# The last two token groups of a feed-forward kernel: their statistics, the flag's test and the last stores put in another order on the vector engine

## The chip, the cores and the metric

The kernel runs on one core of one Trainium2 chip. The metric is the device time of one execution in microseconds (us); less is better. The core has a matrix engine (PE), a vector engine (DVE), an activation engine (ACT), a general engine (POOL) and a synchronisation engine (SP), which here only issues transfers. Each takes its own instructions in order; they wait for one another through semaphores.

## The reference

The input is 4096 tokens of 256 numbers. Cut to what matters:

```python
x = layernorm(x + attn(x))        # linear attention, D = 64
h = silu(x @ w1.T * s1) * (x @ w2.T * s2)     # 256 -> 1024
h = gelu(h @ h1.T * hs1)                      # 1024 -> 1024, exact gelu
h = gelu(h @ h2.T * hs2)
x = layernorm(x + (h @ w3.T) * s3)            # 1024 -> 256; this is the output
```

A layernorm here subtracts the mean of a token's 256 numbers and divides by the root of their variance plus 1e-5. There is no learned scale or shift.

## The kernel before, in words

The tokens are cut into eight tiles of 512, and these are worked on in four pairs. A tile has four groups of 128 tokens (`NS` = 4); within a group a token lies on a partition and its 256 features along the row. Products are made in two parts, of a rounded matrix `hi` and the remainder `lo`, and the square layers use a seven-product scheme. The matrix engine is kept busy with these products from the start to within some 8 us of the end. The program is written out by hand in order: there is no scheduler that moves instructions, so the order of calls in the source is each engine's order.

The change lies in the last stretch, after the last pair's products (`ta` and `tb` are its two tiles). For each group `s` of a tile the work is:

- `last_products` (line 900) makes the group's 128x256 product with `w3` in a PSUM bank;
- `scaled` (line 909) multiplies the bank with `s3` into a tile `d` on the vector engine;
- an addition puts `d` on the residual row `x2[t][:, s, :]`;
- `statistics` (lines 150 and 152) takes mean and variance into `mvo`;
- a reciprocal root of the variance is made. For most groups it is `rstd_of` (lines 87 and 88, with a power on POOL). For the last two groups it is `root_on_act` (lines 1152 and 1153): a square root on ACT, then four small vector steps (reciprocal, and one Newton step of three instructions), which the caller places one by one;
- the row is normalised, either by two ACT instructions (minus the mean, times the root) or by one vector instruction, and stored by `store` (line 1164), a transfer on SP's queue.

The last two groups are `y` (tile `tb`, group 2) and `u` (tile `tb`, group 3). `y` is normalised on ACT (lines 1210 and 1220), `u` on the vector engine (line 1232). Each has a store of its own of 128 KB.

Among these steps stands the end of a test. `within` (lines 1020 and 1021) sets `ok` for the last eight groups' variances, a reduction (line 1225) takes the least of all `ok`, a matrix product with ones (line 1228) adds this over the partitions, and line 1231 turns the sum into `flag`. Four engines load `flag` (line 1234) and branch (line 1240): if it were set, a general program would run again from the start. In the runs here it isn't set.

Of the kernel before, what the change touches and what calls it, by code (L numbers as in the profile page):

```python
# [11 lines left out]
F32 = mybir.dt.float32  # L12
# [4 lines left out]
ALU = mybir.AluOpType  # L17
AX = mybir.AxisListType
# [3 lines left out]
P = 128  # L22
# [8 lines left out]
NS = T // P  # L31
# [13 lines left out]
def block_kernel(ctx: ExitStack, tc: tile.TileContext, a: dict, out: bass.AP):  # L45
# [15 lines left out]
    nc = tc.nc  # L61
# [3 lines left out]
    def const(name, shape, dt=F32):  # L65
        return cp.tile(shape, dt, tag=name, name=name)

    s1 = const("s1", [P, KH])
# [7 lines left out]
    ones = const("ones", [P, 1])  # L76
# [5 lines left out]
    flag = const("flag", [1, 1], I32)  # L82
# [14 lines left out]
    p2 = fast.enter_context(tc.tile_pool(name="two", bufs=2))  # L97
    p3 = fast.enter_context(tc.tile_pool(name="three", bufs=3))

    bank = [bp.tile([P, T], F32, tag=f"bank{i}", name=f"bank{i}") for i in range(8)]  # L100
# [21 lines left out]
    x2 = {}  # L122
# [24 lines left out]
    def norm_stats(us, mv, s0):  # L147
        st = p2.tile([P, 2, 6], F32, tag="bn", name="bn")
        for j, u in enumerate(us):
            nc.vector.bn_stats(st[:, j, :], u)  # L150
        for j in range(len(us)):
            nc.vector.bn_aggr(mv[:, s0 + j, :], st[:, j, :])
# [331 lines left out]
    def sums(layer, k, raw):  # L484
# [20 lines left out]
        def first():  # L505
            plus(v[0], a21, a22)
            plus(v[1], v[0].bitcast(F32), a11, ALU.subtract)
            store(0)

        def second():  # L510
            plus(v[2], a11, a21, ALU.subtract)
            plus(v[3], a12, v[1].bitcast(F32), ALU.subtract)
            store(1)
# [23 lines left out]
    for c in (slice(0, H // 2), slice(H // 2, H)):  # L537
        d = nc.gpsimd.dma_start(out=w1[:, :, c], in_=a["w1"][:, :, c])
# [16 lines left out]
    for _ in range(WARM):  # L555
        nc.tensor.matmul(
            pw, nc.const_aps.tensor(1.0, [P, P], BF), nc.const_aps.tensor(1.0, [P, T], BF),
            start=True, stop=True,
# [232 lines left out]
    for i in range(2, 2 * KH):  # L791
# [13 lines left out]
        if i in (11, 14):  # L805
            t = 2 + i // 14
# [86 lines left out]
    mvo = p1.tile([P, NT * NS, 2], F32, tag="mvo", name="mvo")  # L893
# [12 lines left out]
    def scaled(t, s):  # L906
        ps = (al, be)[t % 2][s]
        d = p2.tile([P, E], F32, tag="d", name=f"d{t}", bufs=4)
        nc.vector.tensor_tensor(d, ps[:, :E], s3, ALU.mult)  # L909
        return d  # L910
# [28 lines left out]
    def end_jobs(t, engine=nc.gpsimd, queue=nc.gpsimd):  # L939
        root, norm, store = out_norm(t)  # L940

        def half(s):
            root([s, s + 1])
            for i in (s, s + 1):
                norm(i, engine)
            if s:
                store(0, NS, queue)

        return [(1.3, functools.partial(half, s)) for s in (0, 2)]
# [45 lines left out]
    low, high, fine, some = (most[:, i : i + 1] for i in range(4))  # L995
    ok = p1.tile([P, NT * NS], F32, tag="ok", name="ok")
# [21 lines left out]
    def within(dst, var, so_far):  # L1018

        nc.vector.tensor_scalar(dst, var, low, so_far, ALU.is_ge, ALU.mult)  # L1020
        nc.vector.scalar_tensor_tensor(dst, var, high, dst, ALU.is_le, ALU.mult)
# [20 lines left out]
    for p in range(NP):  # L1042
        ta, tb = 2 * p, 2 * p + 1
        if p > 0:
            first = []
            ask(1)
            for i in range(2 * KH):
# [13 lines left out]
                if p + 1 < NP and i in (6, 11):  # L1061
                    t = ta + 2 + int(i == 11)
# [77 lines left out]
    def statistics(t, ss):  # L1140
        norm_stats([x2[t][:, s, :] for s in ss], mvo[:, t * NS : (t + 1) * NS, :], ss[0])
# [6 lines left out]
    def root_on_act(t, s):  # L1148

        var, r, e = (p3.tile([P, 1], F32, tag=n, name=n) for n in ("var", "rr", "re"))  # L1150
        mv = mvo[:, t * NS + s, 1:2]
        nc.scalar.activation(r, mv, AF.Sqrt, bias=eps)
        nc.vector.tensor_scalar(var, mv, EPS, None, ALU.add)


        return r, [
            functools.partial(nc.vector.reciprocal, r, r),
            functools.partial(nc.vector.scalar_tensor_tensor, e, r, var, r, ALU.mult, ALU.mult),
            functools.partial(nc.vector.tensor_scalar, e, e, -0.5, 1.5, ALU.mult, ALU.add),
            functools.partial(nc.vector.tensor_tensor, r, r, e, ALU.mult),  # L1160
        ]

    def store(t, s0, s1):
        nc.sync.dma_start(out=out[t][:, s0:s1, :], in_=x2[t][:, s0:s1, :])

    g, v = nc.gpsimd, nc.vector
    for s in range(NS):
# [23 lines left out]
    for s in range(2):  # L1191
        norm_on_act(ta, 2 + s, *ra[s])
    store(ta, 2, 4)
    d = scaled(tb, 1)
    statistics(tb, [0])
    (r0,) = roots(tb, [0])
    y = x2[tb][:, 1, :]
# [6 lines left out]
    store(tb, 0, 2)  # L1204
    n = (NT - 1) * NS
    y, u = x2[tb][:, 2, :], x2[tb][:, 3, :]
    statistics(tb, [2])
    r, steps2 = root_on_act(tb, 2)
    (m,) = minus_mean(tb, [2])
    nc.scalar.activation(y, y, AF.Identity, bias=m, scale=1.0)  # L1210
    d = scaled(tb, 3)
    steps2[0]()
    v.tensor_tensor(u, u, d, ALU.add)
    steps2[1]()
    st = p2.tile([P, 2, 6], F32, tag="bn", name="bn")
    nc.vector.bn_stats(st[:, 0, :], u)
    steps2[2]()
    steps2[3]()
    nc.vector.bn_aggr(mvo[:, n + 3, :], st[:, 0, :])
    nc.scalar.activation(y, y, AF.Identity, scale=r)  # L1220
    store(tb, 2, 3)
    r, steps3 = root_on_act(tb, 3)
    within(ok[:, n - NS :], mvo[:, n - NS :, 1], fine)
    steps3[0]()
    nc.vector.tensor_reduce(some, ok, AX.X, ALU.min)
    steps3[1]()
    pf = bank[7][:1, :1]
    nc.tensor.matmul(pf, some, ones, start=True, stop=True)
    steps3[2]()
    steps3[3]()  # L1230
    nc.vector.tensor_scalar(flag, pf, float(P), None, ALU.is_lt)
    nc.vector.tensor_scalar(u, u, mvo[:, n + 3, 0:1], r, ALU.subtract, ALU.mult)
    store(tb, 3, 4)
    differs = nc.values_load(
        flag, engines=AGAIN, min_val=0, max_val=1,
# [178 lines left out]
```

## Time and profile before

| what | us |
|---|---|
| median of three executions | 638.31 |
| these three | 638.42, 638.31, 636.43 |
| the profiled execution, its own time | 636.66 |
| its span, first to last instruction | 634.8 |
| matrix engine busy | 623.5 |
| last large product ends, from the span's start | about 626.95 |
| last vector instruction, start and length | 630.59, 0.41 |
| last store issued by SP, start and length | 631.03, 0.33 |

The profile shows one execution. Its own time is 1.86 us above its span, which is what lies around the first and the last instruction. Engine rows give start and length, both in us from the span's start. On DVE and ACT, the next instruction can start before the one ahead of it has ended if it doesn't need its result. For SP, a row is the time in which the engine issues a transfer; the landing is told apart from it.

### The profile page before, as it was taken

How to read it: one execution, taken by the hardware profiler on the slowest of the kernel's cores; microseconds unless marked ns; L12 is line 12 of the kernel's file. 1: busy time of each engine (PE TensorE's matmuls, PEld its weight loads, DVE VectorE, ACT ScalarE, POOL GpSimd, SP SyncE). 2: the span in 40 equal slices, each digit the busy share in tenths (PEclk: the TensorE clock that was granted, in tenths of full speed). 3: DMA queues.
4: the chain of work that ended last, by engine and by line, in shares of the span. 5: the costliest groups of instructions: out<-in, count | busy, mean ns of one | idle time of the engine just before them, and what ended most of it. 6: DMA issues, size and time to landing. Idle time of an engine off the chain costs nothing.

```text
span 634.8 us, 9039 instructions
## 1 busy us (share of the span) xinstructions
PE 623.5 (98%) x3169; PEld 526.7 (83%) x3169; DVE 488.4 (77%) x767; ACT 379.2 (60%) x547; POOL 219.0 (34%) x280
## 2 busy tenths in 40 slices
PE   8999999999999999999999999999999999999995
PEld 7788888888898888888898888888898888888894
DVE  2799985889668787889668798798676796597456
ACT  5455553659845374655755457747754547765674
POOL 1343023204855409305545505603653700000043
PEclk9999999999999999999999999999999999999999
DMA  8999669978641158647741135645861035443301
GB/s 340 360 312 319 223 221 359 282 234 257 159 150 65 66 199 291 207 135 219 243 135 33 67 132 190 223 152 176 233 156 35 33 133 174 173 152 132 100 1 69
DMA packets 59409, 113.31 MB, mean 179 GB/s; under 512 B 19776, under 2 KB 34112, under 8 KB 59232
## 3 DMA queue, kind: packets, MB, share of 16 engines
q1 hardware_dynamic: 40880, 73.89, 35.1%
q0 software_dynamic: 18192, 38.41, 19.5%
q8 instruction: 26, 0.43, 0.3%
q10 hardware_dynamic: 288, 0.39, 0.2%
q14 instruction: 23, 0.19, 0.1%
HBM read 96.94 MB, written 18.87 MB: 182 GB/s over the span
## 4 chain that ended last, share of the span: by engine, by line
PE 95%; DVE 2%; DMA 1%; ACT 1%; issue 0%; POOL 0%; ACTq 0%; DVEq 0%; POOLq 0%
PE bank L305 64%; PE bank L737 18%; PE bank L900 9%; PE bank L602 1%; PE bank L140 1%; PE bank L581 1%; DMA f<-in_xt 1%; DVE so L317 0%; DVE bn L150 0%; PE bank L652 0%; PE bank L210 0%; PE bank L747 0%; ACT stk L665 0%; DVE d L909 0%; DVE stk L671 0%
## 5 line engine op out<-in xcount | busy, mean ns | idle before, releaser
L305 PE MATMUL bank<-hi,ws 128*128 128x512 f32 x896 | 348.7, 389 | 0.0
L305 PE MATMUL bank<-lo,ws 128*128 128x512 f32 x896 | 348.6, 389 | 0.0
L260 DVE TENSOR_TENSOR lo<-f,hi 128x1024 fp32r<-128x1024 f32 x142 | 168.3, 1224 | 59.6 <-ACT hi L259 59.0
L305 PEld LDWEIGHTS bank<-lo,ws 128*128 128x128 f32 x896 | 168.2, 188 | 35.0
L305 PEld LDWEIGHTS bank<-hi,ws 128*128 128x128 f32 x896 | 168.1, 188 | 34.9
L259 ACT CAST hi<-f 128x1024 fp32r<-128x1024 f32 x142 | 142.6, 1051 | 48.2 <-PE bank L305 25.1
L355 ACT ACTIVATE f<-f,hs 128x512 f32<-128x512 f32 x96 | 62.5, 715 | 68.7 <-DVE f L317 68.7
L737 PE MATMUL bank<-hi,w 128*128 128x512 f32 (+1 forms) x256 | 99.0, 388 | 0.4 <-ACT hi L218 0.4
L737 PE MATMUL bank<-lo,w 128*128 128x512 f32 (+1 forms) x256 | 98.8, 387 | 0.1
L756 ACT ACTIVATE f<-bank,s 128x512 f32<-128x512 f32 x64 | 44.1, 690 | 68.9 <-PE bank L737 66.0
L317 DVE TENSOR_TENSOR f<-f,f 128x1024 f32<-128x1024 f32 x64 | 76.5, 1221 | 4.5 <-ACT f L355 3.8
L317 DVE TENSOR_TENSOR f<-f,bank 128x512 f32<-128x512 f32 x96 | 61.4, 682 | 15.3 <-ACT f L410 11.3
L757 DVE SCALAR_TENSOR_TENSOR f<-bank,s,f 128x512 f32<-128x512 f32 x64 | 47.8, 748 | 25.2 <-PE bank L737 23.9
L900 PE MATMUL bank<-w,lo 128*128 128x256 f32 x240 | 57.9, 283 | 0.0
L900 PE MATMUL bank<-w,hi 128*128 128x256 f32 x240 | 57.9, 283 | 0.0
L737 PEld LDWEIGHTS bank<-hi,w 128*128 128x128 f32 x256 | 48.1, 188 | 10.1 <-ACT hi L218 0.6
L244 POOL DMA_DIRECT2D xT<-x x96 | 52.2, 551 | 11.7 <-DMA stage<-in_h 4.5
L737 PEld LDWEIGHTS bank<-lo,w 128*128 128x128 f32 x256 | 48.1, 188 | 9.7 <-DVE lo L219 0.3
L862 POOL DMA_DIRECT2D stage<-in_h x16 | 9.2, 575 | 127.2 <-DVE stage L888 100.4
L900 PEld LDWEIGHTS bank<-w,lo 128*128 128x128 f32 x240 | 46.1, 192 | 0.2
L900 PEld LDWEIGHTS bank<-w,hi 128*128 128x128 f32 x240 | 46.0, 192 | 0.2
L915 POOL TENSOR_TENSOR x<-x,d 128x256 f32<-128x256 f32 x29 | 25.7, 904 | 30.8 <-DVE d L909 30.7
(165 smaller groups left out, 538.4 us busy)
## 6 DMA issues: line engine op xcount, KB each, us to landing
ws<-sw SPq DMA_DIRECT2D x100, 512.0 KB, 3.4
sw<-so POOLq DMA_DIRECT2D x16, 512.0 KB, 4.9
stage<-in_h POOLq DMA_DIRECT2D x16, 512.0 KB, 5.0
ws<-in_h POOLq DMA_DIRECT2D x12, 512.0 KB, 6.6
sw<-in_h SPq DMA_DIRECT2D x12, 512.0 KB, 5.5
x<-in_x SPq DMA_DIRECT2D x16, 256.0 KB, 5.6
f<-in_xt SPq DMA_DIRECT2D x7, 512.0 KB, 7.0
f<-in_h SPq DMA_DIRECT2D x6, 512.0 KB, 7.8
```

What stands on the lines that cost most here:

```text
L244: moves.popleft()()
L259: nc.scalar.copy(hi[:, c, :], src[:, c, :])
L260: nc.vector.tensor_tensor(lo[:, c, :], src[:, c, :], hi[:, c, :].bitcast(F32), ALU.subtract)
L305: nc.tensor.matmul(ps[2 * h + o], w[:, k, o * P : (o + 1) * P], part[i][:, k, :], start=start and k == 0 and i == 0, stop=k == HK - 1 and ...
L317: engine.tensor_tensor(dst, u, v, op)
L355: nc.scalar.activation(dst, src, AF.Gelu, scale=sc[:, o : o + 1])
L737: nc.tensor.matmul(ps[:, c], w[:, k, o * P : (o + 1) * P], part[:, 2 * j + k, c], start=(k == 0 and i == 0), stop=(k == KE - 1 and i == 1),)
L756: nc.scalar.activation(g, pa, AF.Silu, scale=s1[:, o : o + 1])
L757: nc.vector.scalar_tensor_tensor(g, pb, s2[:, o : o + 1], g, ALU.mult, ALU.mult)
L862: nc.gpsimd.dma_start(out=st[:, :n], in_=src.rearrange("p k o -> p (k o)")[:, c : c + n])
L900: nc.tensor.matmul(ps[:, :E], part[q][:, k, s * P : (s + 1) * P], w3[:, k0 + k, :], start=i % 2 == 0 and k == 0 and q == 0, stop=i % 2 == ...
L915: engine.tensor_tensor(y[:, s, :], y[:, s, :], scaled(t, s), ALU.add)
```

## The change

The order of the calls for the groups `y` and `u` is rewritten. `u` is scaled and added right behind `y`'s statistics, before `y`'s root. `y`'s and `u`'s statistics get two tiles of their own, `st2` and `st3`. `u`'s square root stands ahead of `y`'s last scaling on ACT. The test (`within`, the reduction, the product) stands ahead of the small steps of the two roots, and these are interleaved. `store` gets a parameter for the queue with SP's as its default, and no call passes another one. No instruction is added or taken out on any engine; the five stores of these two tiles keep their sizes and their order.

```diff
-    def store(t, s0, s1):
-        nc.sync.dma_start(out=out[t][:, s0:s1, :], in_=x2[t][:, s0:s1, :])
+    def store(t, s0, s1, queue=nc.sync):
+        queue.dma_start(out=out[t][:, s0:s1, :], in_=x2[t][:, s0:s1, :])
...
     store(tb, 0, 2)
     n = (NT - 1) * NS
     y, u = x2[tb][:, 2, :], x2[tb][:, 3, :]
-    statistics(tb, [2])
+    st2, st3 = (p2.tile([P, 2, 6], F32, tag="bn", name="bn") for _ in range(2))
+    nc.vector.bn_stats(st2[:, 0, :], y)
+
+    d = scaled(tb, 3)
+    nc.vector.bn_aggr(mvo[:, n + 2, :], st2[:, 0, :])
+    v.tensor_tensor(u, u, d, ALU.add)
     r, steps2 = root_on_act(tb, 2)
     (m,) = minus_mean(tb, [2])
     nc.scalar.activation(y, y, AF.Identity, bias=m, scale=1.0)
-    d = scaled(tb, 3)
+    nc.vector.bn_stats(st3[:, 0, :], u)
     steps2[0]()
-    v.tensor_tensor(u, u, d, ALU.add)
+    nc.vector.bn_aggr(mvo[:, n + 3, :], st3[:, 0, :])
+    r3, steps3 = root_on_act(tb, 3)
+    within(ok[:, n - NS :], mvo[:, n - NS :, 1], fine)
+    nc.vector.tensor_reduce(some, ok, AX.X, ALU.min)
+    pf = bank[7][:1, :1]
+    nc.tensor.matmul(pf, some, ones, start=True, stop=True)
     steps2[1]()
-    st = p2.tile([P, 2, 6], F32, tag="bn", name="bn")
-    nc.vector.bn_stats(st[:, 0, :], u)
+    steps3[0]()
     steps2[2]()
+    steps3[1]()
+    nc.vector.tensor_scalar(flag, pf, float(P), None, ALU.is_lt)
     steps2[3]()
-    nc.vector.bn_aggr(mvo[:, n + 3, :], st[:, 0, :])
     nc.scalar.activation(y, y, AF.Identity, scale=r)
     store(tb, 2, 3)
-    r, steps3 = root_on_act(tb, 3)
-    within(ok[:, n - NS :], mvo[:, n - NS :, 1], fine)
-    steps3[0]()
-    nc.vector.tensor_reduce(some, ok, AX.X, ALU.min)
-    steps3[1]()
-    pf = bank[7][:1, :1]
-    nc.tensor.matmul(pf, some, ones, start=True, stop=True)
     steps3[2]()
     steps3[3]()
-    nc.vector.tensor_scalar(flag, pf, float(P), None, ALU.is_lt)
-    nc.vector.tensor_scalar(u, u, mvo[:, n + 3, 0:1], r, ALU.subtract, ALU.mult)
+    nc.vector.tensor_scalar(u, u, mvo[:, n + 3, 0:1], r3, ALU.subtract, ALU.mult)
     store(tb, 3, 4)
```

## The prediction

> **What bounds the kernel now.** I read the page first, then the chain of waits from its end backwards, then the timelines of DVE, ACT and SP after 626 us, and last the view of the store's line.
>
> ```profile
> PE 623.5 (98%) x3169; PEld 526.7 (83%) x3169; DVE 488.4 (77%) x767; ACT 379.2 (60%) x547; POOL 219.0 (34%) x280
> ...
> PE 95%; DVE 2%; DMA 1%; ACT 1%; issue 0%; POOL 0%; ACTq 0%; DVEq 0%; POOLq 0%
> ```
>
> PE is busy for 98% of the span and carries 95% of the chain. None of that moves. The change stands behind the last product, which ends near 626.95, so it works on the last 7.85 us alone. There the chain runs through DVE, with one step on ACT:
>
> ```profile
> 628.77 0.16 DVE rr L1218
> 628.93 0.10 DVE mvo L1219
> 629.04 0.50 ACT x L1220
> 629.54 0.19 ACT rr L1152
> 629.73 0.02 issue
> 629.75 0.16 DVE rr L1224
> 629.92 0.08 DVE most L1225
> 630.00 0.18 DVE re L1226
> 630.18 0.02 issue
> 630.21 0.17 DVE re L1229
> 630.37 0.02 issue
> 630.40 0.16 DVE rr L1230
> 630.56 0.06 DVE flag L1231
> 630.62 0.39 DVE x L1232
> ```
>
> The reader is to see one detour: the variance of `u` is there at 629.03, but its square root (L1152) stands on ACT behind `y`'s last scaling (L1220), so its reciprocal (L1224) starts at 629.75. The chain stops at 631.0; what follows hangs on SP. In SP's timeline and in the view of the store's line:
>
> ```profile
> 629.56 0.33 SPq L1164 DMA_DIRECT2D out<-x  x1
> ```
>
> ```profile
> 631.03 0.33 SPq L1164 DMA_DIRECT2D out<-x  x1
> DMA to landing us min/median/max: 1.8/2.0/2.0
> ```
>
> `y`'s store goes out 1.47 us ahead of `u`'s, and SP is free when `u` is ready. The lines of the load (L1234) and the branch (L1240) show SP loading the flag at 631.4, just behind this issue, and its closing semaphore waits from 632.5 to 633.1; `u`'s store lands in between, at about 632.9. Both the flag's load and the landing hang on the start of SP's last issue, 3.74 us before the span's end (634.77 less 631.03). So the time is: **start of SP's last issue plus 3.74**.
>
> **What the Trainium skill says.** "Perfetto Trace Analysis", section on the DVE and ACT instruction, says that a row ends where the write is acknowledged and the semaphore is then sent. The trace agrees: a vector instruction that needs the one ahead starts 0.03 to 0.04 after its end (626.50 to 626.53). "VectorE: DVE Perf Modes", section "The DRAIN you can't avoid", says that a next operation that isn't held starts earlier. The trace agrees: 0.33 from start to start behind a 256-wide operation (627.34 to 627.67), 0.07 to 0.08 behind a 128x1, at most 0.13 behind a three-operand one (628.14 to 628.27). "Perfetto Trace Analysis", section on HWDGE transfers, says that SP's row ends when SP is free again, without the movement; here 0.33 against 1.8 to 2.0 to landing. "DMA: Bandwidth & Descriptors", "Anatomy of one DMA", puts most of a small transfer's 2 us down to the receipt of the write; 128 KB and 256 KB landing in 1.8 and 2.0 agrees.
>
> **The change part by part.** Nothing is added: the instructions on each engine are the same in number, and so are the five stores. `queue` is SP's by default in every call, so that edit costs nothing because it changes nothing. The rest is order. I carry the rules above through the new order, with the durations of the DVE and ACT rows.
>
> 1. *`u` scaled at once.* `y`'s `bn_stats` stays at 626.53. The scaling waits for the bank, done at 626.95, so it starts at 626.97 instead of 627.34 and ends at 627.39. `y`'s aggregation goes behind it: 627.30 instead of 627.00 (+0.30). The addition to `u` needs the scaling: 627.42 to 627.85 (before, to 628.22: -0.37). Then var 627.75, minus 627.82; `u`'s `bn_stats` 627.88 to 628.31; `y`'s reciprocal 628.21; `u`'s aggregation 628.34 to 628.52 (before, to 629.03: -0.51).
> 2. *ACT.* `y`'s root at 627.52, `y` minus mean at 628.00 to 628.51, `u`'s root at 628.56 to 628.84. The detour of the chain is gone: the root no longer waits for `y`'s last scaling.
> 3. *The test goes first.* var 628.56, the two of `within` 628.63 and 628.94 to 629.17 (0.28 and 0.23, the second needs the first), reduction 629.21 to 629.37. Before they lay in DVE's wait for ACT; now they stand ahead of both roots, and this takes most of what step 2 won.
> 4. *Woven steps.* `y`'s second step 629.31; `u`'s reciprocal 629.44 to 629.60 (before 629.75: -0.31); `y`'s third 629.57 to 629.71; `u`'s second 629.64 to 629.85; flag 629.76; `y`'s root done 629.84 to 630.00 (before, to 628.93: **+1.07**); `u`'s third 629.92 to 630.07; `u`'s root 630.11 to 630.27; `u` normalised **630.30 to 630.71** (before, to 631.00: **-0.29**).
> 5. *Stores.* `y`'s scaling on ACT waits for two engines and took 0.09 to start (rr ends 628.93, ACT 629.03): 630.10 to 630.61. SP issues `y`'s store at 630.63 instead of 629.56. It is first in SP's queue, so `u`'s, ready at 630.74, waits behind it. An issue takes 0.33, and between two stores stands one semaphore check (the store's line shows two, 17 ns each), with gaps of 0.03 to 0.05: 0.43 in all. `u`'s store goes at **631.06**, against 631.03.
>
> Sum: the vector engine ends 0.29 earlier, and SP's queue gives 0.32 back: **+0.03 us**, so 636.69 for the profiled execution.
>
> Costs that the trace doesn't show. *Two stores back to back*: at least 0.38 (issue and gap alone), at most 0.65, as 0.60 issues of small blocks of xT on this queue; I take 0.43. *Landing of two close stores*: queue 1 spent 35.1% of 16 x 634.8 us on 40,880 packets, 0.087 us each at 1.8 KB; a store is 128 rows of 1 KB, 8 per DMA engine, so at most 0.70 for the first, 0.43 of it past when the second starts: 0 to 0.27 later; I take 0, since a packet here is about half the mean size. A gain I exclude: a second transfer on the same queue has no reason to land faster. *The flag's wait for PE*: behind it on DVE stand the ends of both roots, and ACT and SP behind these. Before, the flag (630.48) followed the reduction's end (630.00) with no wait visible, so PE's answer takes 0.47 at most: 629.84 against my slot of 629.76, 0 to 0.08 late; I take 0. No gain is possible there.
>
> **The rivals.** *(A) SP's queue doesn't bind.* If `y`'s root came 0.3 earlier, the store would be out of the way and the end would be DVE's: -0.29, 636.4. For it: a plain reading of the chain, which ends on DVE. Against it: step 4 puts the test and most of `u`'s steps ahead of `y`'s root. *(B) A jam on SP, slower.* Place: `u`'s store behind `y`'s. It decides once `y`'s store goes later than 630.60 (631.03 less 0.43). Price: the upper bounds, 0.08 + 0.22 + 0.27, on top of 0.03: +0.6, 637.3. If `u`'s store even had to wait for `y`'s landing: 630.63 + 1.85 + 0.03 = 632.51, +1.48, 638.1. Against that last: SP issues the small blocks of xT every 0.65 us while each lands 4.2 later, so the queue doesn't wait for landings. *(C) The change does nothing measurable and the executions' own spread decides.* The four executions shown are 636.43, 636.66, 638.31 and 638.42, 1.99 apart; every price above is smaller.
>
> **How the numbers follow.** Chances: my sum, within 0.15 of no change, 0.55; (A), 0.15; (B), 0.25 up to +0.6 and 0.05 for the landing. All but the last leave the kernel the same; (C) lies over all of them. The profiled execution is 1.65 below the median of the three. Nothing in the tail tells the two pairs apart, so I don't carry the sum to the median: I take the mean of the four executions, 637.46, plus 0.03: **637.5**. Low end 636.43 less 0.23, most of (A): 636.2. High end 638.42 plus 0.4, most of (B): 638.8. Beyond these lie at most 2 in 10. A difference of about 0.3%, 1.9 us, is what a measurement of this kernel can tell from no change. To be faster by that, the median must fall under 636.4: the lower pair with a part of (A), 0.20. To be slower it must pass 640.2: the upper pair with the landing of (B) and more, 0.08. The same: 0.72.
>
> **What would show it.** Right: the last vector row ends near 630.7; `u`'s root on ACT stands ahead of `y`'s scaling; `y`'s store starts near 630.6 and `u`'s 0.4 behind it, near 631.05; the span stays at 634.8 within 0.2. Wrong: `u`'s store with a gap ahead of it on SP (A); an issue gap over 0.65, a landing over 2.1, or the flag later than 629.9 (B); or a span that differs by more than 0.6, which no step of mine explains.

## The result, and the profile after

The changed kernel takes 639.50 us, the median of seven executions (638.36 to 640.45). The kernel before, measured beside it, takes 638.03 (seven executions, 636.43 to 638.66). The ratio is 1.0027, 95% interval 1.0016 to 1.0038: slower by 1.0 to 2.4 us. The forecast was 637.5 within 636.2 to 638.8; the measured time lies above that.

The profiled execution of the changed kernel took 639.76 us with a span of 637.87. Its last large product ends at 628.13 instead of 626.95. That part lies ahead of the changed lines: over the profiles of the nine kernels of this study it ends anywhere from 626.60 to 628.37, and the spread is there as soon as the first stage of products (L581) ends, at 12.4 to 14.2. I therefore measure the **tail**: from the end of the last large product (L900) to the end of the span. It was 7.83 us before and is **9.74** after, 1.91 longer. That is as much as the measured loss, within the interval of 1.0 to 2.4.

The chain of waits of the changed kernel, its last links (start, length, what; all lists below are in us from the span's start):

```profile
630.92 0.14 DVE re L1227
631.05 0.06 DVE flag L1228
631.11 0.07 DVE rr L1229
631.18 0.07 DVE re L1232
631.25 0.02 issue
631.28 0.17 DVE rr L1233
631.45 0.03 issue
631.48 0.41 DVE x L1234
```

No step of ACT stands in it any more, as forecast. The vector engine ends at 631.89, 3.76 behind the last product; before it was 4.06. So DVE gained 0.30. SP's timeline of the changed kernel has the two stores close together, and the view of the store's line shows where the time went:

```profile
631.81 0.33 SPq L1164 DMA_DIRECT2D out<-x  x1
632.24 0.38 SPq L1164 DMA_DIRECT2D out<-x  x1
```

```profile
DMA to landing us min/median/max: 2.0/2.0/3.9
```

`u`'s store is issued 4.11 behind the last product (before 4.09). But the largest landing is 3.9 instead of 2.0. A store has landed when the last of its sixteen semaphore increments has come; the time is counted from its issue. `y`'s store lands in 3.86, `u`'s in 3.74, where the same two took 1.77 and 1.85 before. SP's closing waits stop there, and the span ends 1.89 after the last landing in both kernels.

What else is on the transfer engines then? The transfer view of the kernel before, for the 3.6 us from 629.9 (each figure is a slice of 0.09 us: busy tenths, then GB/s):

```profile
DMA  0000029998200000000001799870047000020000
GB/s 0 0 0 0 0 91 319 364 341 285 57 0 0 0 0 0 0 0 0 0 0 57 250 364 353 285 228 12 0 91 182 0 0 0 0 91 0 0 0 0
q1 hardware_dynamic: 288, 0.26, 21.2%
q14 instruction: 3, 0.02, 2.4%
q8 instruction: 1, 0.02, 1.8%
```

And the changed kernel's, 3.6 us from 632.3:

```profile
DMA  0001899736898510000001401100000000000000
GB/s 0 0 0 57 284 353 501 228 114 250 284 387 296 182 23 11 11 23 0 0 23 23 102 0 23 34 11 11 11 0 11 23 34 23 23 11 0 0 0 0
q1 hardware_dynamic: 288, 0.26, 22.9%
q14 instruction: 3, 0.02, 2.9%
q8 instruction: 1, 0.02, 2.8%
```

Before, there are two separate humps, one for each store, and behind the second one a few isolated slices of 91 or 182 GB/s. Those are packets of the kind "instruction": there are four of them, three of 8 KB and one of 16 KB, and the first one still lies in the end of the second hump. After, the humps have grown together with the instruction packets (the slice of 501), and then a thin stream of 11 to 34 GB/s runs on for two more us. A packet of the stores is 1 KB; one in a slice of 0.09 us is 11 GB/s. So single packets are still trickling out while the rest is done. The record of the semaphores says the same: of `y`'s sixteen increments fifteen come from 633.37 to 633.56, and the last at 635.67. The q8 packet of 16 KB starts at 632.90 and is in work for 1.60 us; before it was 1.04.

By their place in time, it is the engines' branches on the flag that start these packets. Their rows in the kernel before, and in the changed one:

```profile
L1240 ACTq COMPARE_BRANCH  x1: 68/68/68, 631.2 to 631.2; - x1
L1240 PEldq COMPARE_BRANCH  x1: 393/393/393, 631.2 to 631.2; - x1
```

```profile
L1242 PEldq COMPARE_BRANCH  x1: 398/398/398, 631.7 to 631.7; - x1
L1242 ACTq COMPARE_BRANCH  x1: 68/68/68, 631.8 to 631.8; - x1
```

Before, the first instruction packet comes at 632.26, 1.09 after ACT's branch, when the last packets of `u`'s store are on their way (the store was issued 0.15 ahead of that branch). After, PE branches 0.06 ahead of `y`'s issue and 0.49 ahead of `u`'s, and the packets come from 632.90 on, into the middle of both stores. The Trainium skill has a cause for such packets: "Runtime: NRT & Kernel Launch", section "Instruction fetch mechanics", says that a taken branch to a page that isn't loaded forces a DMA fetch of that page. I had not drawn on it. The traces agree in place: in the seven profiles with a branch, the first packet comes 1.08 to 1.24 behind the first branch. They don't say whether a branch was taken. The experiments below take the branch away and move it.

### The profile page after: what moved, and what is told of

It reads as the page before. It is cut to its first block, busy times and chain, and to the rows that moved or that the text cites. A ratio compares the mean times of both kernels' runs of the same rounds, so it can differ in the third digit from the quotient of the medians.

```text
span 637.9 us, 9039 instructions
## 1 busy us (share of the span) xinstructions
PE 625.1 (98%) x3169; PEld 528.2 (83%) x3169; DVE 488.3 (77%) x767; ACT 379.4 (59%) x547; POOL 218.3 (34%) x280
## 4 chain that ended last, share of the span: by engine, by line
PE 96%; DVE 2%; DMA 1%; ACT 0%; issue 0%; POOL 0%; SPq 0%; ACTq 0%; POOLq 0%
PE bank L305 64%; PE bank L737 18%; PE bank L900 10%; PE bank L581 1%; PE bank L602 1%; PE bank L140 1%; DMA f<-in_xt 1%; DVE so L317 0%; PE bank L652 0%; PE bank L210 0%; PE bank L747 0%; ACT stk L665 0%; DVE stk L671 0%; DVE bn L150 0%; POOL ra L88 0%
## 5 line engine op out<-in xcount | busy, mean ns | idle before, releaser
L900 PE MATMUL bank<-w,lo 128*128 128x256 f32 x240 | 57.9, 283 | 0.0
L900 PE MATMUL bank<-w,hi 128*128 128x256 f32 x240 | 57.9, 283 | 0.0
L900 PEld LDWEIGHTS bank<-w,lo 128*128 128x128 f32 x240 | 46.1, 192 | 0.2
L900 PEld LDWEIGHTS bank<-w,hi 128*128 128x128 f32 x240 | 46.0, 192 | 0.2
```

The costliest lines, as they stand in the source:

```text
L900: nc.tensor.matmul(ps[:, :E], part[q][:, k, s * P : (s + 1) * P], w3[:, k0 + k, :], start=i % 2 == 0 and k == 0 and q == 0, stop=i % 2 == ...
```

## The experiments

Three theories went in. Theory 1: the fetches that the branches start hold up the stores. Theory 2: two stores issued closely hold each other up (or, 2b, SP's queue does). Theory 3: the loss is made at the start of the kernel.

**The flag alone moved back.** The changed kernel, with its flag behind `u`'s last scaling:

```diff
     steps3[1]()
-    nc.vector.tensor_scalar(flag, pf, float(P), None, ALU.is_lt)
     steps2[3]()
...
     nc.vector.tensor_scalar(u, u, mvo[:, n + 3, 0:1], r3, ALU.subtract, ALU.mult)
+    nc.vector.tensor_scalar(flag, pf, float(P), None, ALU.is_lt)
     store(tb, 3, 4)
```

> The changed kernel with one instruction moved: the flag (L1228) stands behind u's last scaling, so that the four engines load it and branch about 0.7 us later against the stores. Theory 1 (the branches start fetches of instructions, whose packets of 8 and 16 KB sit on the same DMA engines as the two stores' packets): the fetches then begin behind the stores' packets, both stores land in 1.8 to 2.1 us instead of 3.86 and 3.74, and the tail (from the end of the last large product to the end of the span; 7.83 before, 9.73 after) is 7.8 to 8.1; time about 0.3% under the changed kernel, equal to before within 0.1%. Theory 2 (two stores issued 0.43 us apart on one queue hold each other up): nothing changes, landings 3.7 to 3.9, tail 9.6 to 9.8. Theory 3 (the difference is made at the start of the kernel, not in the tail): the time stays 0.3% over before whatever the tail does.

Measured: 637.90 against 637.93, ratio 1.0001 (0.9990 to 1.0012). The stores are issued at 3.63 and 4.06 behind the last product, 0.43 apart, and land in 1.78 and 1.81. The first branch comes at 4.38, and the tail is 7.79. Its transfer view, 3.6 us from 632.0:

```profile
DMA  0000000028998359995400300703000000000000
GB/s 0 0 0 0 0 0 0 0 80 296 353 353 262 114 194 341 364 364 171 114 0 0 91 0 0 182 0 91 0 0 0 0 0 0 0 0 0 0 0 0
```

Both humps are whole and close together, the first instruction packet comes at the very end of the second one and the other three behind it one by one, and there is no thin stream. One moved instruction gives back everything. Theory 2 falls: the stores are as close as before the move. Theory 3 falls with it.

**No branch at all**, in both orders. The edit is the same in the two kernels; it also takes out the hint for that branch, which the profiles show on four engines at 0.7 to 0.8 us, at the start of the program:

```diff
-    tc.mark_branch_hint_location("again", "LikelyTaken", engines=AGAIN)
...
-    differs = nc.values_load(
-        flag, engines=AGAIN, min_val=0, max_val=1,
...
-    with tc.If(differs > 0, label="again"):
-        general(tc, a, out, locals())
```

> The changed kernel without the load of the flag, the branch and the general program behind it (the guard is left out; the flag is still computed). Theory 1: no fetch is started by a branch on the flag, both stores land in 1.8 to 2.1 us, 0.43 apart, and the tail is under 8. Theory 2: landings stay at 3.7 to 3.9.

> The kernel before without the load of the flag, the branch and the general program (the guard is left out). It gives the order of before without any fetch: u's store lands in 1.8 to 1.9 us as before. By the sum of the prediction the tail of e2_after_no_branch is then longer than this one by 0.0 to 0.1 us; Theory 2 says by 1.8 to 2.0; if the new order by itself gains on the vector engine and SP does not bind, it is shorter by 0.3.

Measured: the changed order 637.01, ratio to before 0.9983 (0.9975 to 0.9990); the order of before 637.07, ratio 0.9985 (0.9977 to 0.9992). `y`'s and `u`'s stores land in 1.96 and 1.92 with the changed order and in 1.97 and 1.87 with the other. The tails are 7.12 and 7.03. Both pages have one packet less on q8 and three less on q14 than that of the kernel before (26 and 23), and none of this kind is left among the last stores:

```profile
q8 instruction: 25, 0.41, 0.3%
q14 instruction: 20, 0.16, 0.1%
```

With the branches gone the two orders are equal within 0.1 us: this is the sum of the prediction, +0.03, and it was right in what it counted. The loss needs the guard. The hint alone can't make it: it stands at the start in all seven kernels with a branch, and the loss comes and goes with the flag's place. Nor does the load of the flag set the packets' time: in the last kernel below, ACT's load takes 0.69 instead of 0.47, and the first packet still comes 1.09 behind ACT's branch, as in the kernel before.

**A store made late in the kernel before.** Two idle instructions hold `u`'s last scaling back, with the flag left where it is:

```diff
     nc.vector.tensor_scalar(flag, pf, float(P), None, ALU.is_lt)
+    for _ in range(2):
+        nc.vector.tensor_tensor(d, d, s3, ALU.mult)
     nc.vector.tensor_scalar(u, u, mvo[:, n + 3, 0:1], r, ALU.subtract, ALU.mult)
```

> The kernel before with two idle multiplications of 128x256 (on d, which nobody reads any more) between the flag and u's last scaling, so that u's store goes out 0.78 us later while the branches stay where they are; y's store is gone 2.2 us earlier. Theory 1: u's store alone falls into the fetches and lands in 2.4 to 4 us instead of 1.85; the tail grows by 0.78 and by 0.6 to 2 more, to 9.2 to 10.6. Theory 2: there is no second store near, so it lands in 1.85 and the tail is 8.6.

Measured: 639.88, ratio 1.0034 (1.0019 to 1.0049). `u`'s store is issued at 4.80 instead of 4.09, and the tail is 10.02: 2.19 longer for 0.71 of delay. The branches of ACT and PE stay within 0.01 of where they were, DVE's comes 0.33 later and SP's, behind the store, 0.71. `y`'s store lands in 1.76; the view of the line has the other one:

```profile
DMA to landing us min/median/max: 1.8/2.0/3.3
```

The order is that of before and the other store is 2.2 us away. A store that is merely late against the branches is held up. This makes the disturbance of the changed kernel in the old one, by 1.47 us instead of 1.89.

**`y`'s store on ACT's queue**, to free SP's:

```diff
-    store(tb, 2, 3)
+    store(tb, 2, 3, nc.scalar)
```

> The changed kernel with y's store on ACT's queue; u's stays on SP's. Rival 2b (the jam on SP's queue is what costs): u's store then goes out 0.3 us earlier, both land in under 2.1 us, and the tail falls from 9.73 to 7.6. Theory 1 (the fetches of instructions that the branches start lie on the same DMA engines whatever queue a store comes from): u's store goes out at 3.8 us behind the last large product instead of 4.1, but at least one of the two still lands in 2.5 to 4 us as long as the branches of PE and DVE stay at 3.6 to 4.0; tail 8.4 to 9.7.

Measured: 639.81, ratio 1.0039 (1.0029 to 1.0049). `u`'s store goes out at 3.78, 0.32 earlier, and nothing is won: the landings are 3.96 and 4.03, and the tail 9.70.

```profile
DMA to landing us min/median/max: 2.0/2.0/4.0
```

Rival 2b falls: it makes no difference here which of the two queues issues `y`'s store. The skill's "DMA: Bandwidth & Descriptors", section "Queues, rings and completion order", has each DMA engine take packets in turn from all the queues with work for it. The trace is in keeping with that, but it doesn't name the engine of a packet, so which engines were shared isn't shown.

This run also shows how the stores are held up. The edit moves ACT's branch 0.96 later, behind its new store, and SP's 0.24 earlier. The 16 KB packet stays at 4.77, which is 0.10 behind ACT's branch and ahead of SP's, so it isn't one of these that brings it. The three packets of 8 KB come only from 5.60 on, when all but a late rest of the stores is through; it is the 16 KB one that the stores meet. It ends at 6.27. No packet of the stores starts from 5.60 to 6.25; then, from 6.26 on, the last eight of each store come in turn. Eight of 128 packets are what each of sixteen engines gets in an even split. It looks as if one engine's share of both stores waited for the end of the 16 KB packet.

**The flag half-way**, directly ahead of `u`'s last scaling:

```diff
+    nc.vector.tensor_scalar(flag, pf, float(P), None, ALU.is_lt)
     nc.vector.tensor_scalar(u, u, mvo[:, n + 3, 0:1], r3, ALU.subtract, ALU.mult)
```

> The changed kernel with the flag directly ahead of u's last scaling: some 0.35 us later than in the changed kernel and 0.3 earlier than in e1_flag_last. Theory 1, as a dose: first branch at about 3.95 behind the last large product (3.61 changed, 4.38 flag last), fetches from 5.0; y's packets (4.4 to 4.9) are through, u's (4.9 to 5.4) meet the fetches in part: y lands in 1.8 to 2.1, u in 2 to 3.5; tail 8 to 9.3. Without a collision: both 1.8, tail 7.8. If only the order of flag and scaling mattered and not the time, it would be as the changed kernel, 9.7.

Measured: 639.54, ratio 1.0027 (1.0009 to 1.0045). The first branch is at 3.92, the first instruction packet at 5.04. `y`'s store, issued at 3.62, lands in 1.77; `u`'s, issued at 4.05, in 4.08. The tail is 10.02, above the 8 to 9.3 that I expected.

```profile
DMA to landing us min/median/max: 1.8/2.0/4.1
```

Here the two stores part. The one that has gone 0.3 ahead of the first branch is untouched, and the one that goes 0.13 behind it pays over 2 us. I had taken the price for a dose that grows with the overlap; it doesn't fit. Fourteen of `u`'s sixteen increments come by 5.86 and the last two at 6.50 and 8.13. Its last packets are two rows of eight: one starts at 5.67, where an 8 KB packet ends, and one at 6.95, where the 16 KB packet ends (6.97). A store is done only with its last increment, so one late share is enough.

**A version meant to beat both.** `y`'s root is finished first, the test stands in the gaps of `u`'s steps, and the flag is last:

```diff
     r3, steps3 = root_on_act(tb, 3)
-    within(ok[:, n - NS :], mvo[:, n - NS :, 1], fine)
...
+    steps2[1]()
+    recent, var8 = ok[:, n - NS :], mvo[:, n - NS :, 1]
+    nc.vector.tensor_scalar(recent, var8, low, fine, ALU.is_ge, ALU.mult)
+    steps2[2]()
+    steps3[0]()
+    steps2[3]()
+    nc.scalar.activation(y, y, AF.Identity, scale=r)
+    store(tb, 2, 3)
+    steps3[1]()
+    nc.vector.scalar_tensor_tensor(recent, var8, high, recent, ALU.is_le, ALU.mult)
+    steps3[2]()
+    nc.vector.tensor_reduce(some, ok, AX.X, ALU.min)
...
+    steps3[3]()
+    nc.vector.tensor_scalar(u, u, mvo[:, n + 3, 0:1], r3, ALU.subtract, ALU.mult)
+    nc.vector.tensor_scalar(flag, pf, float(P), None, ALU.is_lt)
     store(tb, 3, 4)
```

> A version meant to beat both: u scaled at once and its root ahead of y's last scaling, as in the changed kernel, but y's root finished first, the test's two comparisons and its reduction put in the gaps of u's steps, and the flag behind u's last scaling. By the rules of the prediction, counted from the end of the last large product: y's store at 2.9, u's last scaling from 2.9 to 3.3, u's store at 3.35 (before 4.09), flag at 3.4, first branch at 3.95. Theory 1: fetches from 5.0, the stores' packets done by 4.7, both landings 1.8 to 2.0, tail 7.1 (before 7.83), time 0.1% under before, at the edge of what five rounds can tell. If the collision comes from the two stores' closeness (0.43 apart), landings of 3.7 and a tail of 8.9.

Measured: stores at 2.99 and 3.42, landings 1.78 and 1.80, first branch at 4.21, tail 7.14, which is 0.69 under before. The time is 637.56 against 637.23, ratio 0.9996 (0.9985 to 1.0007). The tail does what was expected, though the first branch is 0.26 later than that; the time can't tell it from the kernel before. A gain of 0.69 would be 0.1%, and the interval is as wide as that on either side. It is 0.3% under the changed kernel, if the two ratios are compared.

## Why the prediction was wrong

Steps 1 to 4, the order on DVE and ACT, were right in size. Counted from the last product (626.95 in the prediction, 628.13 in the trace):

| step | predicted | measured |
|---|---|---|
| `u` added, end | 0.90 | 0.92 |
| `u`'s aggregation, end | 1.57 | 1.60 |
| flag, start | 2.81 | 2.84 |
| `y`'s root, end | 3.05 | 3.05 |
| `u` scaled, end | 3.76 | 3.76 |
| `y`'s store issued | 3.68 | 3.68 |
| `u`'s store issued | 4.11 | 4.11 |

Step 5's queueing was right too: 0.43 between the two issues, and what DVE won (0.29 predicted, 0.30 measured) given back on SP.

The step that failed is **the landing of two close stores**, which I bounded by 0 to 0.27 and took as 0. It measured 1.89 (3.74 against 1.85). The bound looked only at what one store does to the other, and that is indeed about nothing: 1.81 with the flag last, 1.92 without a branch. I left out the third party on the DMA engines. The page of the kernel before lists q8 and q14 as "instruction"; that four of their packets lie in the last 3 us stands in the transfer view of the tail, which I looked at only after the result. Two of the signs that I had named came true: a landing over 2.1, and a span that differs by more than 0.6, though 1.2 of its 3.1 lie ahead of the tail.

The second omission is in step 4: I timed the flag and asked only whom it keeps waiting on DVE. The instructions that wait for the flag are four loads and four branches, and the branches were moved 0.69 us ahead on PE, 0.52 on ACT and 0.35 on DVE. `u`'s store stayed where it was within 0.02, so it was the branches that came to it; `y`'s store was itself moved back by 1.06. By the question "what does an earlier step trigger, and what does that collide with", the answer was in the trace: the first branch at 4.23, the first fetch 1.09 later, `u`'s last store packet at 5.38. In the kernel before the first fetch (5.32) already came a little ahead of that packet, and the 16 KB one (5.74) behind it. That its store escaped was a matter of a few tenths: in the half-way kernel a store 0.13 behind the first branch, instead of 0.15 ahead of it, is held up.

Rival (A) was wrong: SP's queue did bind. Rival (B) had the right place and direction and, with its waiting for a landing, nearly the right size (+1.48), but by a mechanism that the runs exclude: `u`'s store was issued 0.43 behind `y`'s, long before `y`'s landed. The size was near by chance. Rival (C), that the spread decides, was wrong: the interval excludes no change. As for the sum `start of SP's last issue plus 3.74`: its 3.74 is a landing of 1.85 plus 1.89 behind it, and only the second stayed (1.89 to 1.92 in the seven profiles with a branch, 1.09 in the two without). Together they were 5.63 after.

What stays open: on which DMA engines the packets meet, why a 16 KB packet takes from 0.95 to 1.60 us, and in part which branch brings which packet. The last 8 KB packet follows SP's branch by 1.08 to 1.18 in all seven profiles with a branch, wherever that branch lies (4.41 to 5.78). The 16 KB packet is not ACT's or SP's; between PE and DVE no run here decides.

## What to carry to other kernels

A flag's branch near the end of a program isn't free when it is hidden: here instruction packets were on the DMA engines 1.1 to 1.2 us later, and a store that met them took about twice as long to land. Set the flag behind the last step that a store waits for, as in the two kernels here with a branch that landed two close stores in 1.8; in the transfer view, check that the humps of the stores are over before the instruction packets begin. When a reordering moves a step forward, list everything that waits for that step on every engine, not only what is behind it on its own, and bound a transfer's landing by all queues in that stretch.

## What the runs showed of the hardware that was not expected

- A 128 KB store that met the instruction packets landed in 3.3 to 4.1 us instead of 1.8 to 2.0 (six stores in four kernels), from SP's queue and from ACT's; in one of them fifteen of sixteen increments were in time and the last came 2.1 us later. In two kernels the late packets are eight of a store, an even share of one engine, and start as an instruction packet ends.
- The load of the flag, the branch and what it fetches cost 0.7 to 0.8 us of the tail even when nothing collides (7.79 and 7.83 with, 7.12 and 7.03 without); without them and their hint, the time is 0.15 to 0.17% under that of the kernel before.
- The nine profiles, one for each kernel, spread by 1.8 us in the first product stage alone: it ends between 12.4 and 14.2, and from there to the last large product all take 614.2 to 614.5.
